# Two graph-attention layers: attention scores with the keys on the partitions and no row maximum, heads in fours, a fixed TensorE order

## The chip, the cores and the metric

The kernel runs on one core of one Trainium2 chip. The metric is the device time of one execution in microseconds (us); runs of a kernel are compared by their median. All data are 32-bit floats.

## What is computed

The input `x` holds 64 graphs of 256 nodes with 512 features; one 0/1 adjacency matrix `adj` (256 x 256) serves all of them. Two layers follow each other, each with a layer norm, a ReLU and a residual.

```python
h = jnp.maximum(_layernorm(x), 0.0)
# layer 0: F1 = 256, one head
hh = h @ W                                    # 512 -> 256
e = leaky_relu(hh @ a[0] + (hh @ a[1]).T, 0.2) + NEG * (1 - adj)
x = x + concat([softmax(e) @ hh, hh], -1)
h = jnp.maximum(_layernorm(x), 0.0)
# layer 1: 8 heads of 64
q, k, v = split_heads(h @ Wq.T + bq), split_heads(h @ Wk.T + bk), split_heads(h @ Wv.T + bv)
s = jnp.where(adj == 0, -inf, (q @ k.T) / 8)
x = x + merge_heads(softmax(s) @ v) @ Wo.T + bo
```

## The kernel before

The 64 graphs are taken in 32 groups of two (512 rows, four row tiles of 128). All weights stay in SBUF. For each group a generator, `Group.before_attention`, does the first layer and the projections; the attention of a group is done while the generator of the next group is advanced in small steps between its pieces. Instructions are written in that order, and a scheduler of the compiler may reorder them on an engine within what the data allow.

The first layer (`layer0`, L197): row statistics on VectorE (L140, L141), `rstd` by a power on GpSimd (L145), the normed rows `xn` (L151), four transposes per row tile into `pt` (L163), ReLU on ScalarE into `hT` (L164); then `ph = hT @ w` (L205, copied to `H` at L209), two transposes `pn` (L217) that spread the neighbour term over partitions, the scores `e` (L223, L227, L228), `exp_rows`, a transpose of the result `pp` (L172) with its copy (L176), and `po` (L237), which L241 adds to `x1`.

`exp_rows` (L178 to L195) works with the queries on the partitions: a row maximum (L184), its negative (L186), one exponential per row tile with the maximum as bias and the row sum as a second result (L189), and the reciprocal of the sums (L194).

`project` makes `q` and `k` with the features on the partitions (L256, evicted by VectorE at L260) and `v` with the nodes on the partitions (L267, L271): twelve products of 128x512 outputs, each of four steps over the 512 features.

The attention of a group goes over eight pairs of heads (4 pairs for each of two graphs). `scores` multiplies `q` and `k` of a pair, each head on its own 64 rows of the array (L307), into the one PSUM tile `sc`; VectorE adds the mask (L314), `exp_rows` follows and L318 divides each row by its sum. `turn` transposes the result by TensorE (L172) and copies it (L176). `weigh` multiplies `v` by it, the two heads in two column halves of the array (L336), and copies the result to `oT` (L341). After four pairs `outputs` applies `wo` (L347), adds to `x1` (L351) and stores (L356, a GpSimd-issued transfer).

PSUM has eight banks of 512 floats per partition: three for `mm` tiles, two for `pp`, two for `sc`, one for `pa`. A 32-bit matmul of the program is two matmul instructions on the engine, a transpose is one.

Of the kernel before, what the change touches and what calls it, by code (L numbers as in the profile page):

```python
# [21 lines left out]

@with_exitstack
def two_gnn_layers(
# [19 lines left out]


# [12 lines left out]
    const = ctx.enter_context(tc.tile_pool(name="const", bufs=1))  # L58
    setup = ctx.enter_context(tc.tile_pool(name="setup", bufs=1))
    big = ctx.enter_context(tc.tile_pool(name="big", bufs=2))  # L60
    att = ctx.enter_context(tc.tile_pool(name="att", bufs=3))
    small = ctx.enter_context(tc.tile_pool(name="small", bufs=6))
    psum = ctx.enter_context(tc.tile_pool(name="psum", bufs=1, space=bass.MemoryType.PSUM))
# [7 lines left out]
    def load(g):  # L71
        t = big.tile([P, GT, D], F32, tag="x", name=f"x{g}", bufs=3)
        nc.sync.dma_start(t, xg[g])
        return t

    loaded = {0: load(0)}
# [13 lines left out]
    loaded[1] = load(1)  # L90
# [44 lines left out]
    def norm_T(src, g, layer, hT):  # L135

        mv = small.tile([P, GT, 2], F32, tag="mv", name=f"mv{layer}_{g}")
        for t in range(GT):
            st = small.tile([P, 6], F32, tag="st", name=f"st{layer}_{g}_{t}")
            nc.vector.bn_stats(st, src[:, t, :])  # L140
            nc.vector.bn_aggr(mv[:, t, :], st)  # L141
        ve = small.tile([P, GT], F32, tag="ve", name=f"ve{layer}_{g}")
        nc.vector.tensor_scalar(ve, mv[:, :, 1], EPS, None, op0=ALU.add)
        rstd = small.tile([P, GT], F32, tag="rstd", name=f"rstd{layer}_{g}")
        nc.gpsimd.tensor_tensor(rstd, ve, rexp, op=ALU.pow)  # L145
        yield
        xn = {}

        def normed(t):
            xn[t] = att.tile([P, D], F32, tag="xn", name=f"xn{layer}_{g}_{t}")  # L150
            nc.vector.tensor_scalar(  # L151
                xn[t], src[:, t, :], mv[:, t, 0:1], rstd[:, t : t + 1],
                op0=ALU.subtract, op1=ALU.mult,
            )

        normed(0)
        for t in range(GT):
            if t + 1 < GT:
                normed(t + 1)
            yield  # L160
            pt = ps(f"pt{layer}_{g}_{t}", "mm", 3).rearrange("p (c t) -> p c t", c=HP)
            for c in range(HP):
                nc.tensor.transpose(pt[:, c, :], xn[t][:, c * P : (c + 1) * P], ident)  # L163
            nc.scalar.activation(hT[:, :, t * P : (t + 1) * P], pt, AF.Relu)  # L164
        yield

    def transposed(p, name):

        pp = ps(f"pp_{name}", "tr", 2).rearrange("p (k q) -> p k q", k=NT)
        for kb in range(NT):  # L170
            for t in range(NT):
                nc.tensor.transpose(  # L172
                    pp[:, kb, t * P : (t + 1) * P], p[:, t, kb * P : (kb + 1) * P], ident
                )
        pT = att.tile([P, NT, N], F32, tag="pT", name=f"pT_{name}", bufs=4)
        nc.scalar.copy(pT, pp)  # L176
        return pT

    def exp_rows(p, mult, name):


        R = p.shape[1]
        mx = small.tile([P, R], F32, tag=f"mx{R}", name=f"mx_{name}")
        nc.vector.reduce_max(mx, p, axis=AX.X)  # L184
        nm = small.tile([P, R], F32, tag=f"nm{R}", name=f"nm_{name}")
        nc.vector.tensor_scalar(nm, mx, -mult, None, op0=ALU.mult)  # L186
        rs = small.tile([P, R], F32, tag=f"rs{R}", name=f"rs_{name}")
        for r in range(R):
            nc.scalar.activation(  # L189
                p[:, r, :], p[:, r, :], AF.Exp, bias=nm[:, r : r + 1], scale=mult,  # L190
                accum_out=rs[:, r : r + 1],
            )
        ri = small.tile([P, R], F32, tag=f"ri{R}", name=f"ri_{name}")
        nc.vector.reciprocal(ri, rs)  # L194
        return ri  # L195

    def layer0(g, x1):  # L197
        xt = loaded.pop(g)
        hT = big.tile([P, HP, TOK], F32, tag="hT0", name=f"hT0_{g}", bufs=1)
        yield from norm_T(xt, g, 0, hT)  # L200
        H = big.tile([P, GT, F1 + 2], F32, tag="H", name=f"H_{g}", bufs=1)
        for t in range(GT):
            ph = ps(f"ph_{g}_{t}", "mm", 3)[:, : F1 + 2]
            for c in range(HP):
                nc.tensor.matmul(  # L205
                    ph, hT[:, c, t * P : (t + 1) * P], w0_sb[:, c, :],
                    start=(c == 0), stop=(c == HP - 1),
                )
            nc.scalar.copy(H[:, t, :], ph)  # L209
            nc.vector.tensor_add(x1[:, t, F1:], H[:, t, :F1], xt[:, t, F1:])  # L210
            yield
        e, ri = {}, {}
        for b in range(GB):

            pn = ps(f"pn_{g}_{b}", "mm", 3)
# [5 lines left out]
            e[b] = att.tile([P, NT, N], F32, tag="e", name=f"e_{g}_{b}", bufs=2)  # L221
# [7 lines left out]
            ri[b] = exp_rows(e[b], 1.0, f"0_{g}_{b}")  # L229
            yield  # L230
        for b in range(GB):
            pT = transposed(e[b], f"0_{g}_{b}")
            yield
            for t in range(NT):
                po = ps(f"po_{g}_{b}_{t}", "mm", 3)[:, :F1]
# [11 lines left out]
    def project(g, x1, q, k, v):  # L247
        hT = big.tile([P, HP, TOK], F32, tag="hT1", name=f"hT1_{g}", bufs=1)
# [3 lines left out]
        for name, dst in (("q", q), ("k", k)):  # L252
            for o in range(HP):
                pq = ps(f"p{name}_{g}_{o}", "mm", 3)
# [9 lines left out]
        for t in range(GT):  # L264
            pv = ps(f"pv_{g}_{t}", "mm", 3)
# [8 lines left out]
    class Group:  # L274
        def __init__(self, g):
            self.g = g
            if g + 2 < NG:
                loaded[g + 2] = load(g + 2)
            self.x1 = big.tile([P, GT, D], F32, tag="x1", name=f"x1_{g}")
            self.q = big.tile([P, HP, TOK], F32, tag="q", name=f"q_{g}")  # L280
            self.k = big.tile([P, HP, TOK], F32, tag="k", name=f"k_{g}")
            self.v = big.tile([P, GT, D], F32, tag="v", name=f"v_{g}")
# [15 lines left out]
        def scores(self, i):  # L298


            b, hp = divmod(i, HP)
            name = f"1_{self.g}_{b}_{hp}"
            sc = psum.tile([P, 2, NT, N], F32, tag="sc", name=f"sc_{name}", bufs=1)
            for t in range(NT):
                for j in range(2):
                    rows = slice(j * DH, (j + 1) * DH)
                    nc.tensor.matmul(  # L307
                        sc[:, j, t, :],
                        self.q[rows, hp, b * N + t * P : b * N + (t + 1) * P],
                        self.k[rows, hp, b * N : (b + 1) * N],  # L310
                        start=True, stop=True,
                    )
            p = att.tile([P, 2, NT, N], F32, tag="p", name=f"p_{name}")
            nc.vector.tensor_add(p, sc, neg1[:, None, :, :].to_broadcast([P, 2, NT, N]))  # L314
            rows = p.rearrange("p j t k -> p (j t) k")
            ri = exp_rows(rows, scale, name)
            for r in range(2 * NT):
                nc.vector.tensor_scalar(  # L318
                    rows[:, r, :], rows[:, r, :], ri[:, r : r + 1], None, op0=ALU.mult
# [3 lines left out]
        def turn(self, i):  # L323
            p = self.p.pop(i)
            self.pT[i] = [transposed(p[:, j], f"1_{self.g}_{i}_{j}") for j in range(2)]

        def weigh(self, i):
            b, hp = divmod(i, HP)
            if i == 0:
                self.oT = big.tile([P, HP, TOK], F32, tag="oT", name=f"oT_{self.g}", bufs=1)  # L330
            pa = ps(f"pa_{self.g}_{i}", "pa", 1)[:, :N]
            pT = self.pT.pop(i)
            for kb in range(NT):
                for j in range(2):
                    c0 = hp * P + j * DH
                    nc.tensor.matmul(  # L336
                        pa[j * DH : (j + 1) * DH, :],
                        self.v[:, b * NT + kb, c0 : c0 + DH], pT[j][:, kb, :],
                        start=(kb == 0), stop=(kb == NT - 1),
                    )  # L340
            nc.vector.tensor_copy(self.oT[:, hp, b * N : (b + 1) * N], pa)  # L341

        def outputs(self, b):
            for t in range(b * NT, (b + 1) * NT):
                py = ps(f"py_{self.g}_{t}", "mm", 3)
# [10 lines left out]
            nc.gpsimd.dma_start(og[self.g][:, r, :], self.x1[:, r, :])  # L356

    pairs = GB * HP
    group = Group(0)
    group.finish()  # L360
    group.scores(0)
    for g in range(NG):
        ahead = Group(g + 1) if g + 1 < NG else None
        for i in range(pairs):
            if ahead is not None:
                ahead.advance(1)
            if i + 1 < pairs:
                group.scores(i + 1)
            elif ahead is not None:
                ahead.finish()  # L370
                ahead.scores(0)
            if ahead is not None:
                ahead.advance(2)
            group.turn(i)
            if ahead is not None:
                ahead.advance(2)
            group.weigh(i)
            if (i + 1) % HP == 0:
                group.outputs(i // HP)
        group = ahead  # L380
# [32 lines left out]
```

## Time and profile before

| | |
|---|---|
| median of 3 runs | 3516.77 us (3516.38 to 3520.48) |
| the profiled execution: its own time | 3516.29 us |
| its span, first to last instruction | 3514.5 us |
| its mean granted TensorE clock | 0.971 of full speed |
| TensorE matmuls busy | 3340.0 us (95%), 13184 instructions |
| VectorE, ScalarE, GpSimd busy | 2026.0 us, 1123.5 us, 259.8 us |

The profile has a page with the busy time of each engine, the span in 40 slices and the costliest groups of instructions; and views that can be asked for: groups by line and shape, the waits, the chain of work that ended last (followed back from the last instruction, each piece with the time by which it advances the chain), a timeline of a window and busy times by window. In groups and timelines, matmuls that overlap are each given their full duration; the chain gives the time by which each run of them moves on. `PE` is TensorE's matmuls, `PEld` its weight loads, `DVE` VectorE, `ACT` ScalarE, `POOL` GpSimd, `SP` the engine that issues most transfers.

### The profile page before, as it was taken

Reading aid. Unit: us, or ns where it says so; the run is one execution under the profiler, and the core shown is the slowest. Engines: PE = TensorE matmul, PEld = TensorE weight load, DVE = VectorE, ACT = ScalarE, POOL = GpSimd, SP = SyncE. Lnnn points to the kernel's source line nnn. Section 1 sums busy time; section 2 is a strip of 40 time slices with the busy share of each in tenths; the row PEclk is TensorE's granted clock in tenths of the full one; section 3 lists DMA queues with packets and bytes.
Section 4 is the critical chain, followed back from the end, with each engine's and each line's share of the span. In section 5 each row is a group of like instructions: output and inputs, shape, how many; then the busy total and the mean of one; then the engine's idle time right before and its main releaser. Section 6 shows DMA issues by size and latency. Waiting matters only on the chain.

```text
span 3514.5 us, 35336 instructions
## 1 busy us (share of the span) xinstructions
PE 3340.0 (95%) x13184; PEld 1825.0 (52%) x13184; DVE 2026.0 (58%) x4247; ACT 1123.5 (32%) x3393; POOL 259.8 (7%) x167
## 2 busy tenths in 40 slices
PE   7999999999999999999999999999999999999998
PEld 4555455555455555455554555445555555555454
DVE  4665555665556655566555665555655556645555
ACT  1333223332233322233322333223332233322233
POOL 0000000000000000000000000000000000000000
PEclk9999999999999999999999999999999999999999
DMA  3000000000000000000000000000000000000000
GB/s 114 19 25 19 12 18 25 25 19 12 25 18 25 19 13 24 18 25 25 7 24 19 24 25 19 13 18 25 24 19 13 24 19 25 19 12 12 7 13 19
DMA packets 30684, 75.15 MB, mean 21 GB/s; under 512 B 2736, under 2 KB 3504, under 8 KB 30512
## 3 DMA queue, kind: packets, MB, share of 16 engines
q1 hardware_dynamic: 21296, 39.33, 3.2%
q0 software_dynamic: 9216, 33.56, 2.5%
q8 instruction: 104, 1.70, 0.2%
q14 instruction: 68, 0.56, 0.1%
HBM read 39.33 MB, written 33.55 MB: 21 GB/s over the span
## 4 chain that ended last, share of the span: by engine, by line
PE 83%; DVE 11%; ACT 4%; issue 2%; DMA 0%; POOL 0%; ACTq 0%; POOLq 0%; DVEq 0%
PE pv L267 13%; PE pq L256 13%; PE pk L256 13%; PE pp L172 9%; PE sc L307 8%; PE pa L336 8%; PE py L347 6%; PE ph L205 6%; DVE mx L184 4%; PE po L237 4%; PE pt L163 2%; DVE nm L186 2%; DVE p L314 2%; ACT p L189 2%; ACT e L223 1%
## 5 line engine op out<-in xcount | busy, mean ns | idle before, releaser
L189 ACT ACTIVATE p<-p,nm 128x256 f32<-128x256 f32 x1024 | 507.4, 497 | 634.5 <-DVE nm L186 634.3
L176 ACT COPY pT<-pp 128x512 f32<-128x512 f32 x576 | 313.3, 583 | 1231.6 <-PE pp L172 1231.3
L256 PE MATMUL pq<-hT,wq_sb 128*128 128x512 f32 x1024 | 448.0, 595 | 34.3 <-ACT hT L164 34.3
L347 PE MATMUL py<-wo_sb,oT 128*128 128x512 f32 x1024 | 462.7, 599 | 0.0
L307 PE MATMUL sc<-k,q 64*128 64x256 f32 x2048 | 397.9, 441 | 67.2 <-DVE p L314 67.2
L267 PE MATMUL pv<-wv_sb,hT 128*128 128x512 f32 x1024 | 461.2, 598 | 0.0
L256 PE MATMUL pk<-hT,wk_sb 128*128 128x512 f32 x1024 | 453.0, 595 | 0.0
L336 PE MATMUL pa<-pT,v 128*64 128x256 f32 x2048 | 354.1, 395 | 2.3 <-ACT pT L176 2.3
L314 DVE TENSOR_TENSOR p<-sc,neg 128x1024 f32<-128x1024 f32 x256 | 312.1, 1219 | 45.7 <-PE sc L307 45.7
L256 PEld LDWEIGHTS pq<-hT,wq_sb 128*128 128x128 f32 x1024 | 191.9, 190 | 278.2 <-issue 229.6
L307 PEld LDWEIGHTS sc<-k,q 64*128 64x128 f32 x2048 | 217.6, 202 | 206.0 <-issue 90.8
L260 DVE TENSOR_SCALAR k<-pk,bk_sb 128x512 f32<-128x512 f32 x128 | 96.1, 751 | 384.3 <-PE pk L256 384.3
L172 PE MATMUL pp<-ident,p 128*128 128x128 f32 x2048 | 315.8, 293 | 1.8 <-DVE p L318 1.5
L267 PEld LDWEIGHTS pv<-wv_sb,hT 128*128 128x128 f32 x1024 | 189.4, 190 | 237.5 <-issue 213.6
L184 DVE TENSOR_REDUCE mx<-p 128x4 f32<-128x1024 f32 x256 | 310.3, 1212 | 3.3
L172 PEld LDWEIGHTS pp<-ident,p 128*128 128x128 f32 x2048 | 251.6, 150 | 109.0 <-issue 81.1
L256 PEld LDWEIGHTS pk<-hT,wk_sb 128*128 128x128 f32 x1024 | 189.6, 190 | 227.2 <-issue 227.2
L318 DVE TENSOR_SCALAR p<-p,ri 128x256 f32<-128x256 f32 x1024 | 299.8, 349 | 4.5
L347 PEld LDWEIGHTS py<-wo_sb,oT 128*128 128x128 f32 x1024 | 186.3, 190 | 212.1 <-issue 202.4
L336 PEld LDWEIGHTS pa<-pT,v 128*64 128x64 f32 x2048 | 145.2, 135 | 178.7 <-issue 81.2
L205 PE MATMUL ph<-w_sb,hT 128*128 128x258 f32 x1024 | 237.3, 384 | 0.0
L271 DVE TENSOR_TENSOR v<-pv,bv_sb 128x512 f32<-128x512 f32 x128 | 88.5, 691 | 249.4 <-PE pv L267 249.4
(49 smaller groups left out, 2705.6 us busy)
## 6 DMA issues: line engine op xcount, KB each, us to landing
x<-in_x_dram SPq DMA_DIRECT2D x32, 1024.0 KB, 5.1
out_dram<-x POOLq DMA_DIRECT2D x64, 512.0 KB, 3.2
wq_sb<-in_L_gnn_Wq_dram SPq DMA_DIRECT2D x1, 1024.0 KB, 11.3
wk_sb<-in_L_gnn_Wk_dram SPq DMA_DIRECT2D x1, 1024.0 KB, 13.4
wv_sb<-in_L_gnn_Wv_dram SPq DMA_DIRECT2D x1, 1024.0 KB, 14.1
wo_sb<-in_L_gnn_Wo_dram SPq DMA_DIRECT2D x1, 1024.0 KB, 15.3
w_sb<-in_L_gnn_W_dram SPq DMA_DIRECT2D x1, 512.0 KB, 7.0
adj_i<-in_adj_dram SPq DMA_DIRECT2D x1, 256.0 KB, 6.1
```

Of the source, the lines that this page charges most:

```text
L172: nc.tensor.transpose(pp[:, kb, t * P : (t + 1) * P], p[:, t, kb * P : (kb + 1) * P], ident)
L176: nc.scalar.copy(pT, pp)
L184: nc.vector.reduce_max(mx, p, axis=AX.X)
L189: nc.scalar.activation(p[:, r, :], p[:, r, :], AF.Exp, bias=nm[:, r : r + 1], scale=mult, accum_out=rs[:, r : r + 1],)
L205: nc.tensor.matmul(ph, hT[:, c, t * P : (t + 1) * P], w0_sb[:, c, :], start=(c == 0), stop=(c == HP - 1),)
L256: nc.tensor.matmul(pq, w_sb[name][:, c, o * P : (o + 1) * P], hT[:, c, :], start=(c == 0), stop=(c == HP - 1),)
L267: nc.tensor.matmul(pv, hT[:, c, t * P : (t + 1) * P], w_sb["v"][:, c, :], start=(c == 0), stop=(c == HP - 1),)
L307: nc.tensor.matmul(sc[:, j, t, :], self.q[rows, hp, b * N + t * P : b * N + (t + 1) * P], self.k[rows, hp, b * N : (b + 1) * N], start=Tru ...
L314: nc.vector.tensor_add(p, sc, neg1[:, None, :, :].to_broadcast([P, 2, NT, N]))
L318: nc.vector.tensor_scalar(rows[:, r, :], rows[:, r, :], ri[:, r : r + 1], None, op0=ALU.mult)
L336: nc.tensor.matmul(pa[j * DH : (j + 1) * DH, :], self.v[:, b * NT + kb, c0 : c0 + DH], pT[j][:, kb, :], start=(kb == 0), stop=(kb == NT - 1),)
L347: nc.tensor.matmul(py, self.oT[:, hp, t * P : (t + 1) * P], w_sb["o"][:, hp, :], start=(hp == 0), stop=(hp == HP - 1),)
```

## The change

`two_gnn_layers` now calls `bounded`, a new form of the whole kernel, and after it `any_inputs`, which is the old form as a loop over the groups, under a condition. `bounded` leaves out every row maximum. A generator `judge` works out from the weights and biases alone (with the fact that a layer norm's row has a length of at most the root of 512) an upper bound on all scores and values, checks that every node has a neighbour, and writes a flag `wrong`; only where it is set does the old form run afterwards.

In `bounded`, scores are computed with the keys on the partitions and the queries along the row, in both layers. The exponential is applied directly, without a bias, and multiplied by the transposed mask `maskT`; no transpose of the result is needed before it multiplies `v`. In the first layer the row sum comes from a column of ones that is appended to `H`. In the second, heads are taken in fours ("quads"): two score tiles of two heads each; GpSimd adds the two key tiles into `ps`; a matmul with `ones` sums `ps` over the partitions; and `weigh` puts each head on one 32-column strip of the array, in two halves of its 64 features. The rows of `wo` are permuted to match. The reciprocal of the sums is applied when the result leaves PSUM.

TensorE's instructions get an explicit chain of dependencies (`in_order`), so that they run in the order in which they are written. Two PSUM banks serve all other products: a "long" product of 128x512 outputs holds one bank, and halfway through it a "short" step of another group's first layer uses the other bank. Four banks hold two `sc` tiles and two the tile `pr`. Three groups are in work: the attention of group g, the projections of g + 1 and the first layer of g + 2; `x` has five buffers. ScalarE now evicts `q` and `k`; GpSimd adds `H` and `bo` to the rows. The core of the diff:

```diff
+def two_gnn_layers(tc, *args):
+    nc = tc.nc
+    with tc.tile_pool(name="verdict", bufs=1) as pool:
+        wrong = pool.tile([1, 1], I32, name="wrong")
+        bounded(tc, *args, wrong)
+        again = nc.values_load(wrong[0:1, 0:1], min_val=0, max_val=1)
+        with tc.If(again > 0):
+            tc.strict_bb_all_engine_barrier()
+            any_inputs(tc, *args)
...
+    turn = {"long": 0, "last": 0, "inside": False}
+    def bank(n, name):
+        turn["last"] = n
+        return psum.tile([P, 512], F32, tag=f"mm{n}", name=name, bufs=1)
+    def mm(name):
+        return bank(1 - (turn["long"] if turn["inside"] else turn["last"]), name)
+    before = []
+    def in_order(instruction):
+        if before:
+            tc.add_manual_dep(
+                instruction.ins, before.pop(),
+                mybir.DependencyInfo(mybir.DependencyClass.NoSync, mybir.DependencyReason.DATA),
+                reason="TensorE's order",
+            )
+        before.append(instruction.ins.name)
+    def matmul(*args, **kwargs):
+        in_order(nc.tensor.matmul(*args, **kwargs))
+    def transpose(*args):
+        in_order(nc.tensor.transpose(*args))
...
+    edge = att.tile([P, NT, N], F32, tag="e", name="edge")
+    nc.vector.tensor_scalar(edge, adj_i, 0.0, None, op0=ALU.not_equal)
+    pt = mm("pt_mask").rearrange("p (k q) -> p k q", k=NT)
+    for kb in range(NT):
+        for t in range(NT):
+            transpose(
+                pt[:, kb, t * P : (t + 1) * P], edge[:, t, kb * P : (kb + 1) * P], ident
+            )
+    nc.vector.tensor_copy(maskT, pt)
...
+                gram = mm(f"gram_{name}{hp}")[:, :P]
+                for c in range(HP):
+                    matmul(
+                        gram, w[:, c, :], w[:, c, :], start=(c == 0), stop=(c == HP - 1)
+                    )
+                a = small.tile([P, P], F32, tag="power", name=f"power_{name}{hp}_0", bufs=1)
+                nc.vector.tensor_mul(a, gram, heads)
+                yield
+                for i in range(3):
+                    square = mm(f"square_{name}{hp}_{i}")[:, :P]
+                    matmul(square, a, a, start=True, stop=True)
...
+    def first_layer(g):
+        xt = xs[g]
+        hT = big.tile([P, HP, TOK], F32, tag="hT0", name=f"hT0_{g}", bufs=1)
+        mv = small.tile([P, GT, 2], F32, tag="mv", name=f"mv0_{g}")
+        for t in range(GT):
+            stats(mv, xt, t, f"0_{g}")
+        yield from norm_T(xt, mv, f"0_{g}", hT)
+        yield
...
+        for t in range(GT):
+            ph = mm(f"ph_{g}_{t}")[:, : F1 + 2]
+            for c in range(HP):
+                matmul(
+                    ph, hT[:, c, t * P : (t + 1) * P], w0_sb[:, c, :],
+                    start=(c == 0), stop=(c == HP - 1),
+                )
+            nc.scalar.copy(H[:, t, : F1 + 2], ph)
+            nc.gpsimd.tensor_add(xt[:, t, F1:], H[:, t, 2 : F1 + 2], xt[:, t, F1:])
+            yield
+        pn = mm(f"pn_{g}")
+        for t in range(GT):
+            transpose(pn[:, t * P : (t + 1) * P], H[:, t, 0:1].to_broadcast([P, P]), ident)
+        pT = {}
+        for b in range(GB):
+            e = att.tile([P, NT, N], F32, tag="e", name=f"e_{g}_{b}")
+            for kb in range(NT):
+                nc.scalar.activation(
+                    e[:, kb, :], pn[:, b * N : (b + 1) * N], AF.Identity,
+                    bias=H[:, b * NT + kb, 1:2], scale=1.0,
+                )
+            nc.vector.scalar_tensor_tensor(e, e, ALPHA, e, op0=ALU.mult, op1=ALU.max)
+            nc.scalar.activation(e, e, AF.Exp)
+            nc.vector.tensor_mul(e, e, maskT)
+            pT[b] = e
+        yield
+        yield
+        mv = small.tile([P, GT, 2], F32, tag="mv", name=f"mv1_{g}")
+        for r in range(GT):
+            b, t = divmod(r, NT)
+            po = mm(f"po_{g}_{r}")[:, : F1 + 1]
+            for kb in range(NT):
+                matmul(
+                    po, pT[b][:, kb, t * P : (t + 1) * P], H[:, b * NT + kb, 2:],
+                    start=(kb == 0), stop=(kb == NT - 1),
+                )
+            ri = small.tile([P, 1], F32, tag="ri", name=f"ri_{g}_{r}")
+            nc.vector.reciprocal(ri, po[:, F1:])
+            nc.vector.scalar_tensor_tensor(
+                xt[:, r, :F1], po[:, :F1], ri, xt[:, r, :F1], op0=ALU.mult, op1=ALU.add
+            )
+            stats(mv, xt, r, f"1_{g}")
+            yield
+        hTs[g] = big.tile([P, HP, TOK], F32, tag="hT1", name=f"hT1_{g}")
+        yield from norm_T(xt, mv, f"1_{g}", hTs[g])
+        for t in range(GT):
+            nc.gpsimd.tensor_add(xt[:, t, :], xt[:, t, :], brow["o"])
+        yield
...
+    def long(name, of, by):
+        turn["long"] = 1 - turn["long"]
+        out = bank(turn["long"], name)
+        for c in range(HP):
+            matmul(out, of(c), by(c), start=(c == 0), stop=(c == HP - 1))
+            if c == HP // 2 - 1:
+                turn["inside"] = True
+                yield
+                turn["inside"] = False
+        return out
...
+        for name, dst in (("q", q), ("k", k)):
+            for o in range(HP):
+                pq = yield from long(
+                    f"p{name}_{g}_{o}", lambda c: w_sb[name][:, c, o * P : (o + 1) * P], lambda c: hT[:, c, :]
+                )
+                nc.scalar.activation(
+                    dst[:, o, :], pq, AF.Identity, bias=bcol[name][:, o : o + 1], scale=1.0
+                )
+                yield
+        for t in range(GT):
+            pv = yield from long(
+                f"pv_{g}_{t}", lambda c: hT[:, c, t * P : (t + 1) * P], lambda c: w_sb["v"][:, c, :]
+            )
+            nc.vector.tensor_add(v[:, t, :], pv, brow["v"])
+            yield
...
+    def scores(g, b, quad):
+        q, k, _ = qkv[g]
+        name = f"{g}_{b}_{quad}"
+        p = att.tile([P, QH, NT, N], F32, tag="p", name=f"p_{name}")
+        ps = att.tile([P, QH, N], F32, tag="ps", name=f"ps_{name}")
+        for i in range(QH // 2):
+            hp = quad * QH // 2 + i
+            sc = psum.tile([P, 2, NT, N], F32, tag="sc", name=f"sc_{name}_{i}", bufs=2)
+            for kb in range(NT):
+                for j in range(2):
+                    rows = slice(j * DH, (j + 1) * DH)
+                    matmul(
+                        sc[:, j, kb, :],
+                        k[rows, hp, b * N + kb * P : b * N + (kb + 1) * P],
+                        q[rows, hp, b * N : (b + 1) * N],
+                        start=True, stop=True,
+                    )
+            pair = p[:, 2 * i : 2 * i + 2]
+            nc.scalar.activation(pair, sc, AF.Exp, scale=scale)
+            nc.vector.tensor_mul(pair, pair, maskT[:, None, :, :].to_broadcast([P, 2, NT, N]))
+            nc.gpsimd.tensor_add(ps[:, 2 * i : 2 * i + 2, :], pair[:, :, 0, :], pair[:, :, 1, :])
+        return p, ps
+    oTs = {}
+    def weigh(g, b, quad, p, ps):
+        v = qkv[g][2]
+        name = f"{g}_{b}_{quad}"
+        if quad == 0:
+            oTs[g, b] = big.tile([P, HP, N], F32, tag="oT", name=f"oT_{g}_{b}")
+        pr = psum.tile([P, 2, 2, N], F32, tag="pr", name=f"pr_{name}", bufs=1)
+        for j in range(QH):
+            matmul(
+                pr[j * S : (j + 1) * S, 1, 0, :], ones[:, :S], ps[:, j, :], start=True, stop=True
+            )
+        r = att.tile([P, N], F32, tag="r", name=f"r_{name}")
+        nc.vector.reciprocal(r, pr[:, 1, 0, :])
+        for half in range(2):
+            for kb in range(NT):
+                for j in range(QH):
+                    c0 = (quad * QH + j) * DH + half * S
+                    matmul(
+                        pr[j * S : (j + 1) * S, 0, half, :],
+                        v[:, b * NT + kb, c0 : c0 + S], p[:, j, kb, :],
+                        start=(kb == 0), stop=(kb == NT - 1),
+                    )
+        nc.vector.tensor_mul(
+            oTs[g, b][:, 2 * quad : 2 * quad + 2, :], pr[:, 0],
+            r[:, None, :].to_broadcast([P, 2, N]),
+        )
+    def outputs(g, b):
+        xt, oT = xs[g], oTs.pop((g, b))
+        for t in range(NT):
+            r = b * NT + t
+            py = yield from long(
+                f"py_{g}_{r}", lambda c: oT[:, c, t * P : (t + 1) * P], lambda c: w_sb["o"][:, c, :]
+            )
+            nc.vector.tensor_add(xt[:, r, :], py, xt[:, r, :])
+            if t == NT - 1:
+                rows = slice(b * NT, (b + 1) * NT)
+                nc.gpsimd.dma_start(og[g][:, rows, :], xt[:, rows, :])
+            yield
+    def run(part):
+        for _ in part:
+            pass
+    def together(part, short):
+        if next(part, none) is none:
+            return
+        next(short, None)
+        next(part, None)
+    none = iter(())
+    run(first_layer(0))
+    first, short = project(0), first_layer(1) if NG > 1 else none
+    for _ in range(3 * HP):
+        together(first, short)
+    run(short)
+    verdict = judge()
+    waiting, late = None, none
+    for g in range(NG):
+        if g + 2 < NG:
+            load(g + 2)
+        projected = project(g + 1) if g + 1 < NG else none
+        short = first_layer(g + 2) if g + 2 < NG else none
+        for b in range(GB):
+            for quad in range(NQ):
+                exps = scores(g, b, quad)
+                if waiting is not None:
+                    weigh(*waiting)
+                    if waiting[2] == NQ - 1:
+                        late = outputs(*waiting[:2])
+                waiting = (g, b, quad, *exps)
+                for _ in range(3):
+                    together(projected, short)
+                    together(late, short)
+                next(short, None)
+                next(verdict, None)
+        run(projected)
+        run(short)
+    weigh(*waiting)
+    run(outputs(*waiting[:2]))
+    run(verdict)
```

The lines of `transposed`, `exp_rows`, the class `Group` and the loop at the end of the old kernel are gone from the path that is run first and remain in `any_inputs`.

## The prediction

> **What bounds the kernel now.** First the page: busy time, then the slices.
>
> ```profile
> PE 3340.0 (95%) x13184; PEld 1825.0 (52%) x13184; DVE 2026.0 (58%) x4247; ACT 1123.5 (32%) x3393; POOL 259.8 (7%) x167
> ...
> PE   7999999999999999999999999999999999999998
> ...
> PEclk9999999999999999999999999999999999999999
> ...
> PE 83%; DVE 11%; ACT 4%; issue 2%; DMA 0%; POOL 0%; ACTq 0%; POOLq 0%; DVEq 0%
> ```
>
> TensorE is full in every slice and carries 83% of the chain; 15% are pieces in which it waits for VectorE or ScalarE. Next the chain in one group's time (start, length, piece), because there each run of matmuls has the time by which it moves on.
>
> ```profile
> 1700.50 1.06 PE sc L307 x8
> 1701.57 7.06 PE pv L267 x16
> 1708.63 0.87 PE pp L172 x8
> ...
> 1732.15 3.49 PE ph L205 x16
> 1735.64 1.01 PE pa L336 x8
> 1736.65 0.38 PE pn L217 x2
> ...
> 1738.71 0.69 DVE e L228
> 1739.40 1.14 DVE p L314
> 1740.53 1.72 DVE mx L184 x2
> ...
> 1743.08 1.97 PE pp L172 x8
> 1745.05 2.01 PE sc L307 x8
> ```
>
> The eight `sc` of a pair take 1.06 us, later 2.01: between them TensorE waited for masks and maxima, and then ran slow. The busy times by window of 1736 to 1744 and 1744 to 1752 (PE, PEld, DVE, ACT, POOL, clock, DMA) show it:
>
> ```profile
> 1736.00:1744.00 8.00, 4.50 (x32) 2.83 (x28) 6.83 (x11) 3.30 (x12) 0.00 (x0) 0.91 0.00 0
> 1744.00:1752.00 8.00, 8.00 (x33) 5.28 (x33) 5.84 (x16) 5.10 (x18) 0.00 (x0) 0.66 0.01 2
> ```
>
> From the starts of single matmuls I take undisturbed paces: 0.429 us for 512 columns, 0.218 for the 258 of `ph`, 0.216 for 256, 0.109 for a transpose. The two heads of an `sc` or `pa` start 7 ns apart and the next two 0.216 us after: two matmuls in one slot. At a change between whole array, row halves and column halves, the first start comes 0.09 us late and the second 0.05 (0.10 into `sc`).
>
> Counted so, the span is 2912 us of streaming; 93 where the order tears the two heads apart (431 slots with one matmul); 132 first and some 85 second late starts (1408 changes); 104 small delays, mostly the slow clock; 160 waits above 0.6 us; 15 before the first matmul, 7 after the last, and 6 of rounding from group means: 3514. The kernel's own time adds 1.8.
>
> **What the Trainium skill says.** "TensorE: Matmul & The Clock Gate", Part 3, has matmuls on different row or column strips run at once, a few ns apart; it gives 2.38 times for three column strips. The trace agrees for two (7 ns); four it never shows. "TensorEngine Tiling (Array Packing)", Key Properties: a change of tiling mode drains the engine; here 0.14 to 0.19 us. Part 1 of the first page says that idle time halves the clock; the trace's 0.66 after a wait agrees. "VectorE: DVE Perf Modes", the walkthrough's hardware budget, has the reciprocal as an iterative divide with a repeat count of 8. The trace has it only at 2 and 4 elements (143 to 179 ns), so for 256 I bound it between a copy of that size (0.42, L341) and, with eight cycles at 0.96 GHz, 2.2 us (an estimate from the page), and take the latter.
>
> **The change, part by part.** *TensorE streaming.* Unchanged are 4096 instructions of 512 columns x 0.429 = 1758, `ph` 1024 x 0.218 = 223, `pt` and `pn` 1152 x 0.109 = 126, and `sc` 1024 slots x 0.216 = 221; `po` gets a 257th column, 512 x 0.217 = 111. All 2304 `pp` transposes go (252). `pa`'s 1024 slots (221) are replaced by `pr`: per quad 16 products on strips and 4 sums, two instructions each, 40; x128 = 5120. If four strips share a slot as two do, that is 1280 x 0.216 = 276. The strips never ran four abreast here: from below the bound is this, since no column streams faster; from above one strip per slot, 1106. I take the former, as 7 ns offsets leave room for four. `judge` adds 112 instructions of 128 columns, 12. Sum **2728**, against 2912 + 93: the fixed order tears no heads apart.
>
> *Changes of tiling.* Per quad whole to rows (0.19), rows to strips (0.14), back (0.14): 0.48 x 128 = **62**, for 217.
>
> *What TensorE waits for in a group.* The fixed order has no other work to slip in. Following the compiled order of each engine through a group, I find two places. (a) Between the last `po` and `pt` of the second norm. VectorE has there: the `py` addition, which must wait for its product; `ve`; three statistics of the next `x` and two aggregates, scheduled ahead; then `xn`. Counting from the last `py` matmul's start: 0.63 until VectorE begins (as q's eviction after pq), 0.67 for the addition, 0.06 `ve`, 3 x 0.59 and 2 x 0.08, then 0.6 until `pt` (0.60 in the first group): 3.85. The power on GpSimd, 1.0, hides in that. TensorE has half a product there, 4 x 0.429, and the end of the one before, 0.43: 2.15. It waits 1.7 us. Everything behind `pt` on TensorE waits with it. (b) After each quad VectorE does mask 1.22, reciprocal 2.2, mask 1.22, `oT` 0.69, from 2.8 us after the quad's first `sc` (first tile 1.06, latency 0.63, exponential 1.0) to 8.1. Behind this queue stands, once a group, the eviction of a `po` (0.15 + 0.48), done at 8.8; its bank is needed by the next product at 8.2 (`sc` 2.0, `pr` 2.3, product 3.4, `po` 0.4): 0.6 us late, nothing if the reciprocal is short. Together 2.3 x 31 = **72**, for the 160 and, as no wait is above 2 us, the 104 too. If the statistics were not ahead, (a) would be 0.3.
>
> *Evictions elsewhere* have half a product (1.72 us) to finish in and need 0.63 + 0.6 (L164) or + 0.74; I count nothing. The cover is gone if an engine is more than 0.4 us behind. The other queues, from rows: VectorE loses maxima, negations, divisions and q/k evictions, and gains the transposed mask at the old price (256 x 1.22) and reciprocals (at most 282): some 1380 us. ScalarE: 256 exponentials of 1024 elements at about 1.0 (from 374 ns at 258 and 583 at 512) replace 1152 at 0.5 and 576 copies; with q and k 256 x 0.6 it has some 690. GpSimd: 4.5 us per 2048 elements (L251) makes 256 sums of 512 x 1.1, `H` additions 128 x 0.6, and `bo` and power as before: some 620. All are half idle. `ps` and mask of a quad are due only a quad later, 16 us on, behind two or three other products; in the last group there is nothing between.
>
> *SP's queue.* `wo` is eight transfers, behind which wait the biases; those are needed from 40 us on, when they have landed (before, `bo` was issued at 19.8). Five buffers of `x` keep loads early. GpSimd's store is queued with its sums: 0.75 each.
>
> *The ends.* The first group: 15 us until the first matmul; then the window 14 to 48 us lost 20 beyond streaming; without maximum and transposes 3 less. The remaining six short steps of group 1's first layer stand alone before the first scores: 5 us of norm (38.0 to 43.0 in the first group) and 2 of evictions. That makes 39. `judge`'s squares stand behind a bank just filled: 36 x 0.3 = 11. The last group has no projections, so its last quad waits for exponential, mask and sum: 7. Then 6.7 as before, and 3 for reading the flag and jumping: no row shows these, from nothing to 10.
>
> Sum: 2728 + 62 + 72 + 39 + 11 + 17 = 2929, the span; with 1.8 it is 2931, and the median stood 0.5 above the profiled time. I say **2931**.
>
> **The rivals.** *Two strips at a time.* The four share something that two don't; then `pr` needs 2560 slots: +276, **3207**. For it: the trace has 54 ns per instruction at the densest (two matmuls and two loads per 0.216), and four abreast needs 27. Against: single loads and matmuls start 2 to 7 ns apart, and a quad's 80 instructions come after products that need only one per 0.215 us, so they can be fetched ahead.
>
> *Waits in all short steps.* A group has 18 of them, each with an eviction to be in time; 0.3 us on each is 18 x 31 x 0.3 = 167, so **3100**. For it: a fixed order turns each lateness into idle time. Against: the slack of 0.4 us and half-idle engines.
>
> *Slower: strips one after the other.* If column strips of 32 don't overlap, 5120 x 0.216 = 1106 in place of 276: **3760**. It decides from where the gain of 586 is used up: spread over 5120 instructions that is 0.114 on top of 0.054 (0.216 / 4), so from 0.168 us between one strip's start and the next. Against it, `pa`'s halves overlap fully.
>
> *The change doesn't do what it says:* the flag is set, and the old form runs too, without overlap between groups, well over 6000 us. From the inputs' definition I worked the bounds out: the scores reach 0.67 (first layer) and 0.76 (second) of the limit, and every node has at least three neighbours. Only a slip in `judge` could do it.
>
> **How the numbers follow.** Forecast 0.72, two strips 0.12, waits 0.10, one after the other 0.04, flag 0.02. The forecast's own spread is 2850 (no wait (a) or (b)) to 3000. With the case of waits, up to 3110, the range holds 0.8; the two-strip case is left out. A measurement tells 0.2%, 7 us. Faster is 0.94, slower 0.05, within 0.01: no case lies near the old time.
>
> **What would show it.** In the profile after: `pr` with 40 instructions in about 2.3 us of chain and `sc` x16 in 1.95; no `pp`; PEclk 1.0 throughout; TensorE's longest repeated wait before `pt` of the second norm, on `xn`, near 1.7 us; `r` near 2.2 us. Wrong would be: `pr` beyond 4 us, waits of TensorE on ScalarE's or VectorE's evictions above 150 us in all, a clock below 0.98, or a second set of lines from the old form.

## The result, and the profile after

The changed kernel takes 3544.44 us (median of 4 runs, 3542.43 to 3545.12) against 3518.44 (median of 4, 3516.38 to 3520.48): a ratio of 1.0073, 95% interval 1.0056 to 1.0090. It is slower by 0.7%, where the forecast was 2931 us. The profiled execution has a span of 3542.1 us and a mean clock of 0.947.

The same lines of the page as before: the busy times, the slices of TensorE and its clock, the chain by engine.

```profile
PE 3025.5 (85%) x14070; PEld 1575.8 (44%) x14070; DVE 1339.2 (38%) x2057; ACT 716.3 (20%) x1131; POOL 702.8 (20%) x684
...
PE   7888888888888888888888888888888888888887
...
PEclk9999999999999999999999999999999999999999
...
PE 74%; DVE 16%; ACT 6%; issue 2%; POOL 2%; DMA 0%; ACTq 0%; DVEq 0%; POOLq 0%
```

TensorE's busy time fell by 315 us, VectorE's by 687 and ScalarE's by 407; GpSimd's rose to 703 us, 20% of the span. And yet the span did not fall. The slices of TensorE, nines before but for the ends, are now eights from end to end, and the chain spends 16% on VectorE, an engine that is busy for 38%. So time seems to go to something that recurs everywhere and that TensorE waits for. The waits of TensorE's matmuls name the candidate (engine, line, waited for: total us, times, longest):

```profile
PE pr L112 <- DVE r L464: 353.9, 128, 4.7
PE pt L115 <- DVE xn L306: 75.5, 35, 5.2
PE pt L115 <- DVE v L421: 30.7, 30, 1.2
PE ph L112 <- ACT q L413: 22.6, 29, 0.8
```

128 is the number of quads. The timeline around one of them shows the order of events (start, length, engine, instruction, in brackets the idle time before and what ended it):

```profile
1736.47 2.00 PE L112 MATMUL sc<-q,k 64*128 64x256 f32 x16
...
1737.71 1.94 ACT L444 ACTIVATE p<-sc 128x1024 f32<-128x1024 f32 x2 [0.54 <-PE sc L112]
...
1738.40 0.64 PE L112 MATMUL pr<-ps,ones 128*32 128x256 f32 x8
1738.77 1.23 DVE L445 TENSOR_TENSOR p<-p,maskT 128x1024 f32<-128x1024 f32 x1 [1.64 <-ACT p L444]
1739.91 1.75 DVE L464 RECIPROCAL r<-pr 128x256 f32<-128x256 f32 x1
```

The products that follow in the same window's TensorE view, and the next product of another group:

```profile
1741.72 3.44 PE L112 MATMUL pr<-p,v 128*32 128x256 f32 x32 [2.68 <-DVE r L464]
1745.09 1.98 PE L112 MATMUL pv<-wv_sb,hT 128*128 128x512 f32 x4
```

TensorE makes the four sums at 1738.40 and is then to multiply `v` by `p`, for which everything has been ready for a quad. It starts at 1741.72, 3.32 us after the sums, when VectorE has finished the reciprocal of these sums; and VectorE came to the reciprocal only after the mask of the next quad, which had waited for the exponential. The products don't read `r`. They write the first half of the tile `pr`, whose second half the reciprocal reads. Then the 32 products take 3.44 us, twice the 1.73 of eight slots of 0.216: the clock is low. The window of 1736 to 1744 (columns as before) has it at 0.84:

```profile
1736.00:1744.00 8.00, 5.32 (x52) 3.06 (x56) 4.52 (x4) 2.54 (x3) 3.89 (x4) 0.84 0.01 2
```

Not every quad is hit like this. The clock records of the trace know only full and half speed. In the changed kernel 104 stretches are at half speed, most of them 3.41 us long and 376 us in all, and they reach the products of 89 of the 128 quads.

**Theory.** TensorE waits in each quad for a reciprocal whose result it doesn't need, because both use one PSUM tile; most of these waits also slow the clock for a while; together this is the difference of 613 us to the forecast, apart from some tens of us. **Rivals.** The fixed order loses time at all its short steps, and this is only where it shows; or the slow clock belongs to the work itself and not to the waits.

### The profile page after: what moved, and what is told of

It is laid out like the page before. It is cut to its first block, busy times and chain, and to the rows that moved or that the text cites. A ratio compares the mean times of both kernels' runs of the same rounds, so it can differ in the third digit from the quotient of the medians.

```text
span 3542.1 us, 33129 instructions
## 1 busy us (share of the span) xinstructions
PE 3025.5 (85%) x14070; PEld 1575.8 (44%) x14070; DVE 1339.2 (38%) x2057; ACT 716.3 (20%) x1131; POOL 702.8 (20%) x684
## 4 chain that ended last, share of the span: by engine, by line
PE 74%; DVE 16%; ACT 6%; issue 2%; POOL 2%; DMA 0%; ACTq 0%; DVEq 0%; POOLq 0%
PE pq L112 13%; PE pk L112 12%; PE pv L112 11%; PE py L112 11%; PE pr L112 10%; PE ph L112 7%; DVE r L464 6%; DVE p L445 4%; ACT p L444 4%; PE pt L115 4%; PE sc L112 3%; PE po L112 3%; DVE st L293 1%; DVE xn L306 1%; POOL rstd L301 1%
## 5 line engine op out<-in xcount | busy, mean ns | idle before, releaser
L112 PE MATMUL pr<-p,v 128*32 128x256 f32 x4096 | 360.5, 512 | 353.9 <-DVE r L464 353.9
L446 POOL TENSOR_TENSOR ps<-p 128x512 f32<-128x512 f32 x256 | 324.8, 1269 | 1093.7 <-DVE p L445 1093.7
L445 DVE TENSOR_TENSOR p<-p,maskT 128x1024 f32<-128x1024 f32 x256 | 306.2, 1196 | 415.9 <-ACT p L444 415.9
L444 ACT ACTIVATE p<-sc 128x1024 f32<-128x1024 f32 x256 | 248.1, 1021 | 290.6 <-PE sc L112 290.6
L112 PE MATMUL ph<-w_sb,hT 128*128 128x258 f32 x1024 | 247.5, 384 | 23.4 <-ACT q L413 22.6
L306 DVE TENSOR_SCALAR xn<-x,mv,rstd 128x512 f32<-128x512 f32 x256 | 154.3, 615 | 293.6 <-PE pt L115 284.3
L115 PE MATMUL pt<-ident,xn 128*128 128x128 f32 x1024 | 165.9, 288 | 107.4 <-DVE xn L306 75.5
L112 PE MATMUL sc<-q,k 64*128 64x256 f32 x2048 | 257.5, 391 | 0.0
L112 PEld LDWEIGHTS ph<-w_sb,hT 128*128 128x128 f32 x1024 | 192.4, 190 | 115.8 <-ACT q L413 46.6
L464 DVE RECIPROCAL r<-pr 128x256 f32<-128x256 f32 x128 | 224.1, 1751 | 1.3 <-PE pr L112 1.3
L112 PEld LDWEIGHTS sc<-q,k 64*128 64x128 f32 x2048 | 188.3, 187 | 70.1 <-issue 48.8
```

The source lines that it names most:

```text
L112: in_order(nc.tensor.matmul(*args, **kwargs))
L115: in_order(nc.tensor.transpose(*args))
L306: nc.vector.tensor_scalar(xn[t], src[:, t, :], mv[:, t, 0:1], rstd[:, t : t + 1], op0=ALU.subtract, op1=ALU.mult,)
L444: nc.scalar.activation(pair, sc, AF.Exp, scale=scale)
L445: nc.vector.tensor_mul(pair, pair, maskT[:, None, :, :].to_broadcast([P, 2, NT, N]))
L446: nc.gpsimd.tensor_add(ps[:, 2 * i : 2 * i + 2, :], pair[:, :, 0, :], pair[:, :, 1, :])
```

## The experiments

Times are medians of 4 runs, ratios are to the kernel before, measured beside each. Nothing but the edit shown differs from the changed kernel, unless the text names a further edit; `...` marks what is left out of a line or between lines.

### Two tiles

```diff
-        pr = psum.tile([P, 2, 2, N], F32, tag="pr", ...)
+        rs = psum.tile([P, 2, N], F32, tag="rs", ...)
+        pr = psum.tile([P, 1, 2, N], F32, tag="pr", ...)
...
-                pr[j * S : (j + 1) * S, 1, 0, :], ones[:, :S], ps[:, j, :], ...
+                rs[j * S : (j + 1) * S, 0, :], ones[:, :S], ps[:, j, :], ...
...
-        nc.vector.reciprocal(r, pr[:, 1, 0, :])
+        nc.vector.reciprocal(r, rs[:, 0, :])
```

> The sums over the partitions go to a PSUM tile of their own, rs, in the bank that was the second half of pr; nothing else changes. Theory (the wait): the products pr<-p,v stand behind the reciprocal r only because both use the tile pr. 128 waits of about 2.85 us (3.32 from the first sum to the first product, less 0.47 for the sums) go, 365 us, and with them most of the slow clock they cause (5.3% of 3542, 187 us at most): 2960 to 3040 us, clock 0.98 or more, no wait of TensorE for r. Rival (the order): the fixed order turns lateness in all short steps into idle time; the place behind the sums is only where it shows, and the idle moves to waits for evictions: 3150 us or more. Rival (the clock): the slow clock comes from the density of the work itself and stays at 0.95: about 3180 us.

Measured: 3029.17 us (3028.73 to 3031.45), ratio 0.8611 (0.8597 to 0.8625), clock 0.989. The number of banks, the instructions and the sizes are the same; the sums only have a tile of their own. The page's row of the products has no idle time left, and a quad in the timeline closes up:

```profile
L112 PE MATMUL pr<-p,v 128*32 128x256 f32 x4096 | 245.3, 379 | 0.0
```

```profile
1707.42 2.00 PE L112 MATMUL sc<-q,k 64*128 64x256 f32 x16
1709.35 0.64 PE L112 MATMUL rs<-ps,ones 128*32 128x256 f32 x8
1709.80 1.91 PE L112 MATMUL pr<-p,v 128*32 128x256 f32 x32
1711.64 1.98 PE L112 MATMUL pq<-hT,wq_sb 128*128 128x512 f32 x4
```

The chain has the same quad without overlaps (start, length, piece):

```profile
1707.49 1.93 PE sc L112 x16
1709.42 0.57 PE rs L112 x8
1709.98 1.73 PE pr L112 x32
```

From sums to products it is now 0.45 us in place of 3.32. 515 us are gone with that wait. As explanations of these 515 us both rivals fall. Idle time did not move to the short steps: the three waits of `pt` and `ph` listed above are 78.2, 31.6 and 22.6 us now, nearly what they were. And the clock came back with the same work: half-speed stretches fall from 376 us to 67, and none reaches a quad's products.

### The sums last

```diff
-        for j in range(QH):
-            matmul(
-                pr[j * S : (j + 1) * S, 1, 0, :], ones[:, :S], ps[:, j, :], start=True, stop=True
-            )
-        r = att.tile([P, N], F32, tag="r", name=f"r_{name}")
-        nc.vector.reciprocal(r, pr[:, 1, 0, :])
         for half in range(2):
...
+        for j in range(QH):
+            matmul(
+                pr[j * S : (j + 1) * S, 1, 0, :], ones[:, :S], ps[:, j, :], start=True, stop=True
+            )
+        r = att.tile([P, N], F32, tag="r", name=f"r_{name}")
+        nc.vector.reciprocal(r, pr[:, 1, 0, :])
```

> Tile pr as in the changed kernel, but in each quad the products pr<-p,v come first and the four sums after them. Theory (the wait): what is waited for is the reciprocal, so with the sums last nothing stands behind it: 2960 to 3040 us as with two tiles, clock 0.98 or more. If the products really waited for the masked p or for another product on VectorE, they would still wait, 2.5 us or more each, and the time stays above 3400 us. If the reciprocal is now late for oT, py waits for oT and some 2 us per graph (128 us) come back.

Measured: 3030.92 us (3029.64 to 3031.33), clock 0.990. One shared tile does no harm if the products are written ahead of the reciprocal. So the wait was for the reciprocal, not for `p` or anything else on VectorE. The waits of `py` for `oT` total 2.3 us, not the 128 allowed for.

### A copy in place of the reciprocal

```diff
-        nc.vector.reciprocal(r, pr[:, 1, 0, :])
+        nc.vector.tensor_copy(r, pr[:, 1, 0, :])
```

> The reciprocal of the sums is replaced by a plain copy of them to r, so the division is left out. Theory (the wait): a copy takes about 0.42 us in place of 1.75, so each of the 128 waits shrinks by 1.33 us, 170 us, and to about 1.5 us; the mask multiplication in front of it on VectorE remains: 3370 us, less by up to 150 if the shorter waits no longer slow the clock. Rival (the order): the wait would hang on something else, and the time changes by less than 50 us.

This kernel leaves the division out. Measured: 3238.80 us (3236.95 to 3240.10), clock 0.985. A timeline of one quad:

```profile
1508.17 0.64 PE L112 MATMUL pr<-ps,ones 128*32 128x256 f32 x8
1508.54 1.22 DVE L445 TENSOR_TENSOR p<-p,maskT 128x1024 f32<-128x1024 f32 x1 [1.64 <-ACT p L444]
1509.68 0.42 DVE L464 COPY r<-pr 128x256 f32<-128x256 f32 x1
...
1510.15 1.93 PE L112 MATMUL pr<-p,v 128*32 128x256 f32 x32 [1.35 <-DVE r L464]
```

The products start 1.98 us after the sums, 1.34 sooner, and take 1.93 us, at full clock. The time falls by 306 us: 171 for the shorter waits (354 to 183 us in all), and the rest, some 135, with the clock. With gaps of 2.0 us between sums and products a half-speed stretch reaches the products of 2 quads, with 3.3 us those of 89.

### The wait filled with work

```diff
         nc.vector.reciprocal(r, pr[:, 1, 0, :])
+        junk = mm(f"junk_{name}")
+        for _ in range(3):
+            matmul(junk, w_sb["q"][:, 0, :P], w_sb["k"][:, 0, :], start=True, stop=True)
```

> The changed kernel with its shared tile pr and its wait, but between the sums and the products of each quad TensorE computes three products of 512 columns that nobody uses (wq by wk into a free bank): 6 x 0.429 us and two changes of tiling, 2.86 us in a gap of 2.85. Theory (wait plus clock): of the 515 us between the changed kernel and two tiles, 365 are the waits themselves and 150 the slow clock after them. The filler takes the place of the idle time and leaves the 365, but keeps the clock: 3390 to 3430 us, clock 0.98 or more. Rival: the 150 are something else that the wait brings (late evictions, queues): 3510 us or more, since nothing is waited for less.

Measured: 3412.97 us (3408.85 to 3415.57), clock 0.987. Adding six matmul instructions per quad to the changed kernel makes it faster by 131 us:

```profile
1515.44 0.64 PE L112 MATMUL pr<-ps,ones 128*32 128x256 f32 x8
1516.01 2.84 PE L112 MATMUL junk<-wk_sb,wq_sb 128*128 128x512 f32 x6
1518.78 1.93 PE L112 MATMUL pr<-p,v 128*32 128x256 f32 x32
```

Sums to products is 3.34 us, much as in the changed kernel, but the products take 1.93 us, and no half-speed stretch reaches them. This divides the 515 us: 131 are the slow clock, and 384 (3413 less 3029) are the 128 gaps, 3.0 us each on the mean.

### Without the fixed order

```diff
-        if before:
+        if False and before:
             tc.add_manual_dep(...)
```

> The chain of dependencies that fixes TensorE's order is left out; the compiler's scheduler orders TensorE by its own estimates, and puts half a product of another group between the sums and the products of most quads. Theory (the wait): the wait behind the sums shrinks by that half product, 1.72 us of 2.85 in most quads: about 200 us and part of the slow clock, 3200 to 3340 us, and some torn pairs of heads. Rival (the order): it is the fixed order as such that costs, and without it the time falls below 3100 us.

Measured: 3044.20 us (3043.46 to 3044.63), clock 0.995. I had expected 3200 to 3340; below 3100 was what I had given to the rival that the order itself costs. The compiler's scheduler puts products of other groups between sums and products:

```profile
1522.84 0.64 PE L112 MATMUL pr<-ps,ones 128*32 128x256 f32 x8
1523.41 1.98 PE L112 MATMUL pq<-hT,wq_sb 128*128 128x512 f32 x4
...
1526.15 1.93 PE L112 MATMUL pr<-p,v 128*32 128x256 f32 x32 [0.55 <-DVE r L464]
```

The products still start 3.31 us after the sums, but most of that time is used, and the waits of `pr` for `r` fall from 354 us to 76.7. So two edits take the loss away almost equally, a separate tile in the fixed order (3029) and a free order with the shared tile (3044): the loss of 515 us needs both, the false wait and an order that has nothing to put in front of it.

> Two tiles for sums and products, and no chain that fixes TensorE's order. Without the chain the changed kernel took 3044 us with some 78 us of waits in front of pr; those go: 2960 to 2990 us. If the fixed order were worth having once the false wait is gone, this stays above the 3029 of two tiles with the chain.

Measured, with both edits: 2920.53 us (2920.32 to 2922.05), 40 less than the least expected. In the free order the false wait still costs 124 us (3044 less 2921), a quarter of what it costs in the fixed one. And two tiles in the fixed order take 109 us more than this, so the first rival is right about a smaller part: the fixed order does lose time at its short steps. The next runs look there.

### Two repairs in the fixed order

To two tiles in the fixed order are added a step between the last `po` and the second norm of a group, and for the short step ahead of the scores the bank of the step before:

```diff
             stats(mv, xt, r, f"1_{g}")
             yield
+        yield
...
-        return bank(1 - (turn["long"] if turn["inside"] else turn["last"]), name)
+        return bank(1 - (turn["long"] if turn["inside"] or turn["steady"] else turn["last"]), name)
...
+                turn["steady"] = True
                 next(short, None)
+                turn["steady"] = False
```

> Two tiles and the fixed order, with two repairs at the waits that are left: one more step of another group lies between the last po and the second norm of a group's first layer, and the short step ahead of the scores uses the other bank, not that of the product that just ended. Left with two tiles are about 104 us where pv is followed by pt, and 27 where pq is followed by ph; the rest of the sum stands as forecast. Theory: 2900 to 2945 us, clock 0.99. Rival: the waits only move to the next short step: above 3000 us.

Measured: 2904.22 us (2903.25 to 2904.64), ratio 0.8252 (0.8238 to 0.8266), clock 0.995. The page's busy line and slices:

```profile
PE 2829.5 (97%) x14070; PEld 1537.5 (53%) x14070; DVE 1339.9 (46%) x2057; ACT 715.9 (25%) x1131; POOL 744.9 (26%) x684
...
PE   6899999999999999999999999999999999999998
```

> Two tiles and the fixed order with one more step before the second norm, and without the other bank. The wait of ph for the eviction of pq (27 us in the trace of two tiles) is left, so 2904 + 27, about 2931 us; if the step alone makes the whole gain, 2904.

Measured, with two tiles and the step alone: 2938.65 us (2936.24 to 2939.59). So the step is worth 90 us, and the bank, added to it, 34.

> Two tiles, the step and the bank, and no chain that fixes TensorE's order. What is left to gain for a scheduler is small, and it tears heads apart and changes the tiling more often (about 16 + 33 us more in the trace without the chain than with it): 2910 to 2940 us against 2904, so that the fixed order is worth some 10 to 30 us once nothing waits in it.

Measured, with two tiles and both repairs and without the chain: 2902.32 us (2901.26 to 2903.92), ratio 0.8245 (0.8231 to 0.8259), the same as with the chain within the spread of the runs. The 10 to 30 us that I gave the fixed order are not there: once its waits are mended it is as good as the scheduler's, and no better.

### Without the bound check

From two tiles, `judge`, the flag and the old form are left out.

```diff
-        again = nc.values_load(wrong[0:1, 0:1], min_val=0, max_val=1)
-        with tc.If(again > 0):
-            ...
...
-    verdict = judge()
+    verdict = none
```

> Two tiles, without the bound check, the flag and the old form behind it. The check was costed at 12 us of matmuls, 11 of waits and 3 for the flag: 26 us less than two tiles, 2995 to 3010. If the mere presence of the old form in the program costs something at fetching instructions, more than 50 us go.

Measured: 3000.63 us (2997.91 to 3000.81), 28.5 less than two tiles; 26 had been costed. If that cost is right, the unused old form adds no more than a few us by being there; no run parts the two.

## Why the prediction was wrong

**The step that failed** is "What TensorE waits for in a group": "Following the compiled order of each engine through a group, I find two places." There is a third, in every quad, which the sum put at nothing without a reason: the products `pr<-p,v` wait for the reciprocal of the sums. The prediction had its parts. In (b) it lists VectorE's queue after a quad, mask, reciprocal, mask, `oT`, with a price for each; but it asked only what stands behind that queue once a group, the eviction of a `po`, and not which of TensorE's instructions stands behind the reciprocal in every quad. Two tiles show the missing term, 515 us, and the filled wait divides it, 384 us idle and 131 by the clock. With it the sum would have been 2931 + 515 = 3446. The other 98 us are what two tiles (3029) take above the forecast; about half of them are the short steps' waits, 122 us after the first 60 us where the sum has 72.

**The forecast's sign rested on that.** "The fixed order has no other work to slip in" was right, and is the reason why one overlooked wait of 2.9 us cost its full length 128 times. Two of the signs that the prediction had named for being wrong came with it: waits of TensorE for VectorE and ScalarE of 483 us in the four lines above, not under 150, and a clock below 0.98.

**The clock.** "PEclk 1.0 throughout" failed with the wait. The Trainium skill's statement that idle time halves the clock ("TensorE: Matmul & The Clock Gate", Part 1) is borne out by the filled wait: the same products at the same place take 1.93 us, not 3.44, when junk precedes them. The prediction had struck out the 104 us of slow clock "as no wait is above 2 us"; with the missed wait this fell too, and even two tiles have 67 us at half speed.

**Wait (a)** was mis-sized: 1.7 us in the sum, 53 us in all; the trace has 2.06 on `xn`. In the whole run the waits for `xn` are 75.5 us, 65 of them after the first 60 us, the rest belonging to the ends. At another step comes a wait of 0.78 on the eviction of `pv`, 30.7 us in all, which I had costed at nothing. A view of all engines shows the wait for `xn` in order:

```profile
1726.37 1.29 DVE L293 BATCH_NORM_STATS2 st<-x 128x6 f32<-128x512 f32 x2
1726.66 0.59 PE L112 MATMUL py<-wo_sb,oT 128*128 128x512 f32 x1
...
1727.65 0.66 DVE L486 TENSOR_TENSOR x<-py,x 128x512 f32<-128x512 f32 x1
...
1728.61 0.73 POOL L489 DMA_DIRECT2D out_dram<-x  x1 [2.81 <-DVE ve L299]
1729.36 1.04 POOL L301 TENSOR_TENSOR rstd<-ve,rexp 128x4 f32<-128x4 f32 x1
...
1729.64 0.66 DVE L293 BATCH_NORM_STATS2 st<-x 128x6 f32<-128x512 f32 x1
1730.44 1.00 DVE L306 TENSOR_SCALAR xn<-x,mv,rstd 128x512 f32<-128x512 f32 x2
1731.04 1.02 PE L115 MATMUL pt<-ident,xn 128*128 128x128 f32 x4 [2.06 <-DVE xn L306]
```

From the last `py` matmul to `pt` it is 4.38 us; the prediction's terms give 3.89 (it writes 3.85). The larger part of the difference is the start of the `py` addition, 0.99 us after that matmul in place of 0.63, because two statistics were still under way on VectorE. A smaller part is the store, a step that I named but did not place: GpSimd issues it just ahead of the power, so the power ends at 1730.40, and `xn` starts 0.14 us after the last statistics. The power did not hide behind them by that much. No run tests this apart.

**Wait (b)**, 0.6 us for the eviction of a `po`, is not there: the changed kernel's list of waits has none, two tiles a single one of 0.8. The sum allowed for that "if the reciprocal is short", and it took 1.75 us, not 2.2. In its place stands one of `ph` for the eviction of `q`, 22.6 us, in the short step outside a product, where the bank is that of the product just ended; the wait of `pt` for `pv` is of the same kind. The bank experiment removed 34.

**What held.** The streaming. Four strips share a slot: 32 products take 1.73 us in the chain of two tiles, eight slots of 0.216, so the rivals "two strips at a time" and "one after the other" fall. `sc` x16 takes 1.93 against 1.95 foretold. The bound check (28.5 against 26) and the loads of VectorE and ScalarE (1339 and 716 us against some 1380 and 690) are near; GpSimd's, 703 against 620, is further off. With the tile parted and the waits of the short steps mended the kernel reaches 2904 us, 27 below the forecast, but that nearness is in part luck. Most of the 72 us of (a) and (b) is mended away there, and without them the sum is 2859: some 45 us are in terms that it put too low. In the trace of that run 16 us of waits for `xn` are left after the first 60 us; the rest stays open.

**The rivals as stated** did not contain what happened. "Waits in all short steps" had the right kind of loss, lateness that a fixed order turns into idle time, in the wrong place and at a third of its size (167 us against 515); the slower rival had the right sign by a mechanism that is refuted.

## What to carry to other kernels

When an order is fixed by hand, go through it wait by wait and ask of each which instruction it is for, whether the data need it or only the tile, and what that engine does first; a wait of 3 us in each of 128 rounds, with the clock that it cost, undid a change that saves 14% without it. Give what is read by one engine a tile of its own when another engine writes beside it, or write the reader behind the writer; here either took the whole 515 us away. And where TensorE idles for some us again and again, count the clock as well: here it added a third to the idle time.

## What the runs showed of the hardware

- With gaps of 3.3 us from sums to products in each quad the products ran at half clock, wholly or in part, in 89 of 128 quads (mean clock 0.947); with gaps of 2.0 us in 2 (0.985). The half-speed stretches were mostly 3.41 us long. Matmuls that nobody needs, put into the gaps, made the kernel 131 us faster.
- Four 32-column strips ran abreast without loss: 32 matmuls in 1.73 us of chain, one per 54 ns, in blocks of 40 with their loads.
- A reciprocal of 256 elements per partition from PSUM took 1.75 us. The prediction's 2.2 us was an estimate of eight cycles for each, from the repeat count of 8 in the Trainium skill ("VectorE: DVE Perf Modes", the hardware budget); the measurement is below it.
